# Graph attention with edges sorted on the chip: rows in a ring, earlier requests, scores by absolute values, sums per chunk and ScalarE weights in the last chunk

## Chip, core and metric

The kernel runs on one core of one Trainium2 chip. The metric is the device time of an execution in microseconds. Of the kernel before, three timed runs gave 5407.89, 5410.82 and 5411.46 us (median 5410.82). One more execution was profiled.

## What is computed

One graph-attention layer over 12,500 nodes of 128 features and 412,500 edges of 64 features. The core of the reference (biases, the layer norm ahead of it and the second norm behind it are left in one line each):

```
h0 = relu(layernorm(x))
h, q, k, v = h0 @ Wn, h0 @ Wq, h0 @ Wk, h0 @ Wv          # + biases
eh = edge_features @ We
hmid   = leaky_relu(concat([q[src], k[tgt], eh]) @ A1 + b1, 0.2)
scores = leaky_relu(hmid @ A2 + b2, 0.2)                   # 8 heads per edge
w   = softmax(scores.mean(-1), axis=0)                     # over ALL edges
out = segment_sum(w[:, None] * v[tgt], src)                # by source node
y = h + out
result = x + gamma * layernorm_core(y) + beta
```

The target nodes of the edges come sorted, the source nodes don't. The softmax runs over all edges at once, and the sum goes by source node.

## The kernel before

**Tiling.** Nodes lie in 98 blocks of 128. Edges lie in 403 groups of 8 tiles of 128, cut into four chunks of 121, 109, 98 and 75 groups (CHUNKS, line 62). For each chunk there is a table in HBM (`tabs`) in which every node block has 11, 10, 9 or 7 tiles of 128 edge rows; a row holds the place of its source node within the block, 128 hidden values and 128 values of v (ROW = 257 float32).

**First stage** (`first_stage`, line 757): for every group, matmuls make the rows of its edges (lines 809 and 812), ScalarE takes them out of PSUM into a ring of 16 rows (lines 792 and 795), and POOL stores them with indirect DMAs into the table at slots counted beforehand (line 747). Counting and placing (`count`, `plan`, `place_slots`) run beside the chunk before.

**Second stage** (`second_stage`, line 824): for every node block of a chunk,
- `load` (831): SP asks for the block's rows (`rows_of`, at most 11 tiles, a pool of BUFS = 6 buffers) and for `qw`, the block's query rows.
- `places` (839): PE transposes the places into `t_bank`; `put_places` (843): ScalarE makes them bytes (`plT`) and stores them to HBM; `spread_places` (850): SP loads them back broadcast to all partitions (`pls`); `select` (857): VectorE makes the one-hot matrix `sel_q`.
- per quad of 4 tiles, `turn` (864): PE transposes the hidden rows and adds the query part; `steep` (876): leaky ReLU, as ScalarE's `low` = 0.2 h (881) and VectorE's maximum (882), which writes back into `rows_of`.
- `heads_of` (885): PE multiplies by A2 into `s_ps`; `add_bias` (893): ScalarE, `z`; `by_slot` (898): VectorE's leaky ReLU of z (902) and its transpose (904); `scores` (906): `none` (910, marks empty slots), the sum over heads (912), score and its maximum (916).
- `spread_top` (919), `greatest` (928): the largest score so far, over all partitions; `exponentials` (933); `add_weights` (945): this block's sum, faded by the change of the maximum (948).
- `weights` (951): VectorE makes, for each tile, the matrix `w` with the edge's weight at its source's place (955); `products` (959): PE multiplies it with the v part (964); `add_sums` (967) adds the result into `acc` (971, 973).

**The order of the work.** PE, VectorE, ScalarE and SP each run in the order in which the instructions are written (a manual schedule), and `plan_of` (line 976 on) sets that order. A block of nq quads begins at step t = 2 i0, i0 being the number of quads before it: a block of 9 to 11 tiles has three quads and so six steps, a block of 7 tiles has two quads and four steps. Each job has a step relative to t and, within a step, a turn value. The products of a block run LAG = 11 steps behind its turns. Steps of the second stage are interleaved with those of the first stage of the next chunk (`interleave`, `some_steps`); the stage of chunk c's stores runs beside the second stage of chunk c - 1, and the second stage of the last chunk runs alone. SP's loads stand in the same order: a load whose wait isn't met stops all that are behind it.

**Setup.** Line 227 on: A2 and b2 are loaded and divided by 8; `b2_col` holds the bias at partitions 32 g to 32 g + 7. Line 246 on: src and dst are loaded (`raw_src`, `raw_dst`), and all slots come from them.

**End.** `all_sums` (1020) turns the per-block sums into one; the last lines normalize and store. `other_edges` (1035) treats edges that found no slot; there its loop runs zero times.

Of the kernel before, what the change touches and what calls it, by code (L numbers as in the profile page):

```python
# [10 lines left out]
FP = mybir.dt.float32  # L11
# [3 lines left out]
U8 = mybir.dt.uint8  # L15
AF = mybir.ActivationFunctionType
ALU = mybir.AluOpType
AX = mybir.AxisListType
# [4 lines left out]
P = 128  # L23
D = 128
DE = 64
H = 8
EPS = 1e-5
SLOPE = 0.2
# [5 lines left out]
QUAD = 4  # L34
LAG = 11

BUFS = 6

RROWS = 16

SPARE = 2

# [8 lines left out]
ROW = 2 * D + 1  # L51
# [60 lines left out]
def kernel(ctx: ExitStack, tc: tile.TileContext, n_edges, x, src, dst, ea, w_nv, w_qt, w_kt,  # L112
# [12 lines left out]
    nc = tc.nc  # L125
    NP = x.shape[0]
    NTN = NP // P
# [8 lines left out]
    for i, share in enumerate(CHUNKS):  # L136
        n = NG - g0 if i == len(CHUNKS) - 1 else max(1, round(NG * share))
# [4 lines left out]
    NC = len(chunks)  # L142
    most_tiles = max(ct for _, _, ct, _ in chunks)

    blocks = []
# [24 lines left out]
    late = ctx.enter_context(tc.tile_pool(name="late", bufs=1))  # L170
# [60 lines left out]
    nc.vector.memset(b2_col, 0.0)  # L231
    for g in range(4):
        nc.scalar.dma_start(out=b2_col[32 * g:32 * g + H, :], in_=b2.rearrange("a h -> h a"))
    nc.vector.tensor_scalar(a2_sb, a2_sb, 1.0 / H, None, op0=ALU.mult)
    nc.vector.tensor_scalar(b2_col, b2_col, 1.0 / H, None, op0=ALU.mult)


    w_ea = const.tile([P, 2, D], FP, name="w_ea")
    cp = ctx.enter_context(tc.tile_pool(name="count", bufs=2))
# [410 lines left out]
    sums_of = late.tile([P, NTN], FP, name="sums_of")  # L650
    nc.vector.memset(sums_of, 0.0)

    def newest(top_of, old, new, pool):

# [169 lines left out]
    def second_stage():  # L824


        rows_of, qws, plss, state = {}, {}, {}, {}
        state["s_ps"] = ps_s.tile([P, 512], FP, name="s_ps")
        nc.vector.memset(state["s_ps"], 0.0)

        def load(i):
            c, b, ct, _, _ = blocks[i]
            rows_of[i] = pb.tile([P, most_tiles, ROW], FP, name="rows_of")
            nc.sync.dma_start(out=rows_of[i][:, 0:ct, :],
                              in_=tabs[c % 2][b * ct * P:(b + 1) * ct * P, :].rearrange("(p j) r -> p j r", p=P))
            qws[i] = ps.tile([P, 3 * D], BF, name="qw")
            nc.sync.dma_start(out=qws[i], in_=q_tab.rearrange("(p t) d -> t p d", p=P)[b])
# [4 lines left out]

        def put_places(i):
            ct = blocks[i][2]
            plT = p3.tile([most_tiles, P], U8, name="plT")
            nc.scalar.activation(plT[:ct, :], t_bank[:ct, 0:P], AF.Copy)
            at = i % 4 * most_tiles
            nc.scalar.dma_start(out=pl_d[at:at + ct, :], in_=plT[:ct, :])
# [49 lines left out]
        def by_slot(i):  # L898

            n = 32 * blocks[i][2]  # L900
            z = state["z"][:, 0:n]
            nc.vector.scalar_tensor_tensor(z, z, SLOPE, z, op0=ALU.mult, op1=ALU.max)
            state["zt"] = p3.tile([P, most_tiles * 32], FP, name="zt")
            nc.vector.transpose(state["zt"][:, 0:n], z)
# [28 lines left out]
        def exponentials(i):  # L933
            c, b, ct, _, _ = blocks[i]
            score = state["score", i][:, 0:ct]
            less = less_of[c % 2][:, b:b + 1]
            if c == 0:
                nc.scalar.activation(score, score, AF.Exp, bias=less, accum_out=sums_of[:, b:b + 1])  # L938
            else:
                state["part", i] = ps.tile([P, 1], FP, name="part_of")  # L940
                nc.scalar.activation(score, score, AF.Exp, bias=less, accum_out=state["part", i])
# [3 lines left out]
        def add_weights(i):  # L945
            c, b, _, _, _ = blocks[i]
            if c > 0:
                nc.vector.scalar_tensor_tensor(sums_of[:, b:b + 1], sums_of[:, b:b + 1], state["fade", i],
                                               state.pop(("part", i)), op0=ALU.mult, op1=ALU.add)

        def weights(i, q):
            state["w", i, q] = ws = []
            for t in range(q * QUAD, min((q + 1) * QUAD, blocks[i][2])):
                w = pw.tile([P, P], FP, name="w")
                nc.vector.tensor_scalar(w, iota_f, rows_of[i][:, t, 0:1], state["score", i][:, t:t + 1],  # L955
                                        op0=ALU.is_equal, op1=ALU.mult)
                ws.append(w)

        def products(i, q):
            ct = blocks[i][2]  # L960
# [17 lines left out]
        def at(when, turn_, job, *args):  # L978
            plan_of.setdefault(when, []).append((turn_, len(plan_of[when]) if when in plan_of else 0, job, args))

        for i, (c, b, ct, nq, i0) in enumerate(blocks):
            t = 2 * i0
            at(load_at(i), 2, load, i)
            first = t - 9 if nq > 2 else t - 8
            at(first, 3, places, i)
            at(first + 1, 0, put_places, i)
            at(first + 3, 0, spread_places, i)
            at(t - 1, 3, select, i)
            for q in range(nq):
# [12 lines left out]
            for q in range(nq):  # L1002
                at(t + 2 * q - 1, 0, weights, i, q)
                at(t + 2 * q, 1, products, i, q)
            at(t + 2 * nq - 1, 0, add_sums, i)
        for when in range(min(plan_of), max(plan_of) + 1):
            for _, _, job, args in sorted(plan_of.get(when, []), key=lambda j: j[:2]):
                job(*args)
            yield

    def load_at(i):

        _, _, _, nq, i0 = blocks[i]
        t = 2 * i0 - (17 if nq > 2 else 11)
        if i >= BUFS:
            _, _, _, nq, i0 = blocks[i - BUFS]
            t = max(t, 2 * (i0 + nq - 1) + LAG)
        return t

    def all_sums():  # L1020

        less = less_of[(NC - 1) % 2]
        most_of = late.tile([P, NTN], FP, name="most_of")
        nc.vector.tensor_scalar(most, less[:, NTN - 1:NTN], -1.0, None, op0=ALU.mult)
        nc.scalar.activation(most_of, less, AF.Exp, bias=less[:, NTN - 1:NTN], scale=-1.0)
        nc.vector.tensor_mul(sums_of, sums_of, most_of)
        nc.vector.tensor_reduce(sums, sums_of, AX.X, ALU.add)
        return most_of

    def count_left():  # L1030
# [4 lines left out]
    def other_edges(most_of):  # L1035

        with tc.tile_pool(name="others", bufs=1) as op, tc.tile_pool(name="others_ps", bufs=1, space=PSUM) as ops_:
            turns = nc.values_load(trips[0:1, NC:NC + 1], min_val=0, max_val=NG, skip_runtime_bounds_check_because=BECAUSE)
            with tc.For_i(0, turns, 1) as g:  # L1039
                b2_bc = op.tile([P, H], FP, name="b2_bc")  # L1040
                nc.sync.dma_start(out=b2_bc, in_=b2.to_broadcast([P, H]))
                nc.vector.tensor_scalar(b2_bc, b2_bc, 1.0 / H, None, op0=ALU.mult)
# [53 lines left out]
                nc.vector.scalar_tensor_tensor(z, z, SLOPE, z, op0=ALU.mult, op1=ALU.max)  # L1096
                sc = op.tile([P, SUPER], FP, name="sc")
                nc.vector.tensor_reduce(sc, z, AX.X, ALU.add)
                none = op.tile([P, SUPER], FP, name="none_n")
                nc.vector.tensor_scalar(none, flag, 1e30, -1e30, op0=ALU.mult, op1=ALU.add)  # L1100
                nc.vector.tensor_add(sc, sc, none)
# [23 lines left out]
    for c in range(NC + 1):  # L1125
# [16 lines left out]
        if c == 0:  # L1142
# [3 lines left out]
                    pass  # L1146
            clear_rest(1)
            setup.close()
            pb = main.enter_context(tc.tile_pool(name="pb", bufs=BUFS))
# [97 lines left out]
```

## Time and profile before

| what | value |
|---|---|
| median of three timed runs | 5410.82 us |
| the profiled execution | 5393.0 us |
| its span, first to last instruction | 5391.3 us |
| busy share of the span: PE, DVE, ACT, POOL | 78%, 78%, 40%, 63% |
| mean granted TensorE clock | 0.921 |
| L747 indirect stores on POOL | 3223, 3343.9 us, mean 1038 ns |
| L955 weights on VectorE | 3626, 1037.2 us, mean 356 ns |
| L902 leaky ReLU of z on VectorE | 392, 180.5 us, mean 461 ns |
| L948 faded sums on VectorE | 294, 64.8 us, mean 220 ns |
| L881 `low` on ScalarE | 1078, 569.0 us, mean 528 ns |
| moved by DMA | 1309.97 MB, mean 243 GB/s |

How to read it: an engine's busy time is the union of its instructions, so durations of instructions that overlap add up to more. A group's idle time is what its engine waited ahead of it, with the releaser behind the arrow. "issue" is idle time in which nothing that the profile shows was waited for. In the timeline the columns are start, duration, engine, line and operation; "x3" merges three neighbours. Shares over the whole span hide the stages, which have different limits, so tables by window are read first. Waits of SP (SPq) are those of the queue that issues the loads.

### The profile page before, as it was taken

What the parts mean: (1) busy time and instruction counts of PE and PEld (TensorE: products, weight loads), DVE (VectorE), ACT (ScalarE), POOL (GpSimd) and SP (SyncE); (2) the same over time, 40 slices, a digit from 0 to 9 for tenths busy, and PEclk for the clock granted to TensorE, in tenths of its full rate; (3) what the DMA queues carried; (4) which work ended last, traced back from release to release, by engine and by line L of the source; (5) the groups of instructions that cost most, each with busy time, mean ns of one, the idle gap of its engine ahead of it and who ended that gap; (6) DMA issues with size and microseconds to landing.
All of it is one profiled execution on the core that took longest, in us unless ns stands there. A gap on an engine that the chain in (4) does not pass through costs nothing. (4 is left out here: it accounts for less than half of the span.)

```text
span 5391.3 us, 90152 instructions
## 1 busy us (share of the span) xinstructions
PE 4218.1 (78%) x26817; PEld 2951.6 (55%) x27160; DVE 4204.3 (78%) x13299; ACT 2160.8 (40%) x6046; POOL 3379.1 (63%) x3261
## 2 busy tenths in 40 slices
PE   4777766565588888998788888987888888878782
PEld 2344433333266666666566666665666666655551
DVE  7777754544378888888788988887877788799889
ACT  1344422222244444444344444443444444434333
POOL 0477777777677777777667777777666666500002
PEclk8788887777789999999999999999999999999996
DMA  8677765555489999888789999988899998755554
GB/s 244 201 234 228 230 196 162 169 164 167 162 262 290 280 280 282 279 281 281 251 257 284 289 284 282 282 286 260 263 284 280 276 287 284 242 194 193 190 194 164
DMA packets 609678, 1309.97 MB, mean 243 GB/s; under 512 B 117392, under 2 KB 371524, under 8 KB 571168
## 3 DMA queue, kind: packets, MB, share of 16 engines
q1 hardware_dynamic: 404312, 841.81, 53.1%
q0 software_dynamic: 154704, 424.26, 21.8%
q10 hardware_dynamic: 50168, 38.07, 2.2%
q8 instruction: 218, 3.57, 0.3%
q14 instruction: 276, 2.26, 0.1%
HBM read 782.14 MB, written 521.60 MB: 242 GB/s over the span
## 5 line engine op out<-in xcount | busy, mean ns | idle before, releaser
L747 POOL DMA_INDIRECT tab<-row,slots x3223 | 3343.9, 1038 | 1339.5 <-issue 702.8
L809 PE MATMUL row_ps<-w_ea,ea_t 128*128 128x256 f32 x3224 | 1105.0, 427 | 379.2 <-ACT row L795 311.5
L964 PE MATMUL o_ps<-rows_of,w 128*128 128x128 f32 x7252 | 1073.6, 287 | 127.9 <-DVE w L955 125.7
L964 PEld LDWEIGHTS o_ps<-rows_of,w 128*128 128x128 f32 x7252 | 954.8, 193 | 254.7 <-DVE w L955 199.7
L795 ACT ACTIVATE row<-row_ps 128x512 f32<-128x512 f32 x1612 | 939.6, 590 | 279.7 <-PE row_ps L812 215.7
L955 DVE TENSOR_SCALAR w<-iota_f,rows_of,score 128x128 f32<-128x128 f32 x3626 | 1037.2, 356 | 0.8 <-ACT score L938 0.8
L809 PEld LDWEIGHTS row_ps<-w_ea,ea_t 128*128 128x128 f32 x3224 | 577.9, 208 | 680.9 <-ACT row L795 397.7
L881 ACT ACTIVATE low<-h_ps 128x512 f32<-128x512 f32 (+3 forms) x1078 | 569.0, 528 | 848.7 <-PE h_ps L873 690.8
L873 PE MATMUL h_ps<-sel_q,qw 128*128 128x512 bf16 (+3 forms) x2891 | 753.7, 344 | 60.1 <-DVE sel_q L861 40.2
L882 DVE TENSOR_TENSOR rows_of<-h_ps,low 128x512 f32<-128x512 f32 (+3 forms) x1078 | 648.2, 601 | 134.7 <-ACT low L881 121.3
L812 PE MATMUL row_ps<-kv,sel 126*128 126x256 bf16 x3224 | 666.3, 290 | 1.5 <-DVE sel L785 1.5
L792 ACT ACTIVATE row<-place 128x4 f32<-128x4 bf16 x806 | 166.9, 207 | 1219.5 <-DMA tab<-row,slots 1195.7
L870 PE MATMUL h_ps<-ident,rows_of 128*128 128x128 f32 x3626 | 592.9, 279 | 0.0
L450 DVE TENSOR_TENSOR one<-bins_b,block 128x500 f16<-128x500 bf16 x646 | 301.5, 467 | 326.8 <-PE run L457 322.8
L812 PEld LDWEIGHTS <-sel 126*128 126x128 bf16 x3224 | 337.6, 105 | 279.3 <-issue 55.0
L870 PEld LDWEIGHTS h_ps<-ident,rows_of 128*128 128x128 f32 x3626 | 433.1, 143 | 102.2 <-issue 39.5
L503 DVE TENSOR_REDUCE num<-run 128x5 f32<-128x500 f32 x646 | 433.4, 671 | 11.8 <-PE run L457 11.8
L861 DVE TENSOR_SCALAR sel_q<-pls,part 128x1408 bf16<-128x1408 uint8 (+3 forms) x392 | 330.6, 843 | 108.5 <-DMA pls<-pl_d 108.0
L1174 POOL TENSOR_TENSOR xt<-xt,affine 128x640 f32<-128x640 f32 (+1 forms) x20 | 32.7, 1649 | 608.2 <-DMA xt<-in_x 595.4
L873 PEld LDWEIGHTS <-qw 128*128 128x128 bf16 x3234 | 314.9, 99 | 160.7 <-issue 54.6
L889 PE MATMUL s_ps<-rows_of,a_sb 128*32 128x352 f32 (+3 forms) x3136 | 292.2, 444 | 117.2 <-DVE rows_of L882 116.1
L457 PE MATMUL run<-one,rest_b 128*128 128x500 f16 x642 | 268.9, 419 | 145.1 <-DVE num L503 143.9
(195 smaller groups left out, 4161.9 us busy)
## 6 DMA issues: line engine op xcount, KB each, us to landing
rows_of<-tab SPq DMA_DIRECT2D x98, 1413.5 KB
rows_of<-tab SPq DMA_DIRECT2D x98, 1285.0 KB
rows_of<-tab SPq DMA_DIRECT2D x98, 1156.5 KB
ea_t<-in_ea SPq DMA_DIRECT2D x403, 256.0 KB
rows_of<-tab SPq DMA_DIRECT2D x98, 899.5 KB
tab<-row,slots POOLq DMA_INDIRECT x3223
offs<-off_d SPq DMA_DIRECT2D x403, 126.0 KB
tab<-blank SPq DMA_DIRECT2D x196, 257.0 KB
```

The lines of the kernel that those rows point to most:

```text
L503: nc.vector.tensor_reduce(num, strips[:, :, :m].rearrange("p b m -> p m b"), AX.X, ALU.max)
L747: i = nc.gpsimd.indirect_dma_start(out=tabs[c % 2][:, :], out_offset=bass.IndirectOffsetOnAxis(ap=slots[c][t // (8 * STR)][:m, t % (8 * ST ...
L795: nc.scalar.activation(row[:, :, 1:ROW], bank, AF.Copy)
L809: nc.tensor.matmul(bank[:, :, 0:D], lhsT=ea_g[:, ts(k, P)], rhs=w_ea, start=True, stop=False, skip_group_check=True)
L812: nc.tensor.matmul(bank[:, b, :], lhsT=sel[:, ts(b * halves + k, P)], rhs=kv, start=False, stop=True, skip_group_check=True)
L861: nc.vector.tensor_scalar(sel[:, 0:n], plss[i][:, 0:n], part1, None, op0=ALU.is_equal)
L870: nc.tensor.matmul(h_ps[:, ts(j, P)], lhsT=rows_of[i][:, q * QUAD + j, 1:D + 1], rhs=ident, is_transpose=True, start=j == 0, stop=False, s ...
L873: nc.tensor.matmul(h_ps[:, 0:m * P], lhsT=qws[i][:, ts(k, D)], rhs=plss[i][:, q * QUAD * P:(q * QUAD + m) * P], start=False, stop=k == 2, ...
L881: nc.scalar.activation(low, h_ps, AF.Copy, scale=SLOPE)
L882: nc.vector.tensor_max(rows_of[i][:, q * QUAD:q * QUAD + m, 1:D + 1], h_ps.rearrange("p (j e) -> p j e", j=m), low.rearrange("p (j e) -> p ...
L955: nc.vector.tensor_scalar(w, iota_f, rows_of[i][:, t, 0:1], state["score", i][:, t:t + 1], op0=ALU.is_equal, op1=ALU.mult)
L964: nc.tensor.matmul(state["o_ps"][:, 0:D], lhsT=w, rhs=rows_of[i][:, t, D + 1:ROW], start=t == 0, stop=t == ct - 1)
```

## The change

1. Rows of the second stage lie in one tile of 66 tile places, `held`, used as a ring, instead of six buffers of 11 tiles: 66 places hold 6 blocks of 11 or 10 tiles, 7 of 9, 9 of 7. `load_at` asks for them at step -19 (three quads) or -17 (two quads), not before the places are free, instead of -17 or -11.
2. `places` goes to step -11 and `put_places` to -10 for all blocks (from -9 and -8, or -8 and -7); `spread_places` goes to -6 (three quads, as before) or -7 (two quads, from -5). `plT` gets two buffers.
3. The leaky ReLU of the scores is replaced: with slope s, the sum over heads of leaky(z) equals (1-s)/2 times [sum of |z| + (1+s)/(1-s) times sum of z]. A2 and b2 are scaled by (1-s)/2 and get a ninth column H with the second sum, so VectorE's L902 goes, the sum over heads takes absolute values, and one addition of column H to `none` comes in. The bias column is now made from a row by a matmul into `t_bank`.
4. Softmax sums: each block's sum is kept, and they are joined once per chunk (`sum_chunk`) instead of once per block (L948).
5. In the last chunk the weights of tiles 1, 3 and 5 of a block's 7 are made by ScalarE in two activations, |iota - place| and then relu(score - 4 |iota - place|).
6. For blocks of two quads `heads_of` moves from step t-1 (turn value 3) to step t (turn value 2, behind the next block's first turn), and all jobs from `add_bias` to `exponentials` come one step later; t is the step behind the last turn.

The diff, cut to its core:

```diff
-BUFS = 6
+RING = 66
+PEAKS = (1, 3, 5)
...
+    bend, line = (1.0 - SLOPE) / 2.0, (1.0 + SLOPE) / (1.0 - SLOPE)
+    nc.vector.tensor_scalar(a2_sb, a2_sb, bend / H, None, op0=ALU.mult)
+    nc.vector.tensor_reduce(a2_sb[:, H:H + 1], a2_sb[:, 0:H], AX.X, ALU.add)
+    nc.vector.tensor_scalar(a2_sb[:, H:H + 1], a2_sb[:, H:H + 1], line, None, op0=ALU.mult)
...
+    with tc.tile_pool(name="bias_row", bufs=1) as bp:
+        b2_row = bp.tile([1, 4, 32], FP, name="b2_row")
+        nc.vector.memset(b2_row, 0.0)
+        for g in range(4):
+            nc.scalar.dma_start(out=b2_row[:, g, 0:H], in_=b2)
+        nc.vector.tensor_scalar(b2_row, b2_row, bend / H, None, op0=ALU.mult)
+        nc.vector.tensor_reduce(b2_row[:, :, H], b2_row[:, :, 0:H], AX.X, ALU.add)
+        nc.vector.tensor_scalar(b2_row[:, :, H], b2_row[:, :, H], line, None, op0=ALU.mult)
+        nc.tensor.matmul(t_bank[:, 0:1], lhsT=b2_row.rearrange("p g h -> p (g h)"), rhs=ones[0:1, 0:1], start=True, stop=True)
+        nc.vector.tensor_copy(b2_col, t_bank[:, 0:1])
...
+    def sum_chunk(c, most_in):
+        less = less_of[c % 2]
+        nc.scalar.activation(most_in, less, AF.Exp, bias=less[:, NTN - 1:NTN], scale=-1.0)
+        if c > 0:
+            fade = late.tile([P, 1], FP, name="fade_sums")
+            nc.scalar.activation(fade, less_of[1 - c % 2][:, NTN - 1:NTN], AF.Exp, bias=less[:, NTN - 1:NTN], scale=-1.0)
+        nc.vector.tensor_mul(sums_of[c % 2], sums_of[c % 2], most_in)
+        part = late.tile([P, 1], FP, name="part_sums")
+        nc.vector.tensor_reduce(part if c > 0 else sums, sums_of[c % 2], AX.X, ALU.add)
+        if c > 0:
+            nc.vector.scalar_tensor_tensor(sums, sums, fade, part, op0=ALU.mult, op1=ALU.add)
...
+        held = pb.tile([P, RING, ROW], FP, name="rows_of")
...
-            rows_of[i] = pb.tile([P, most_tiles, ROW], FP, name="rows_of")
+            rows_of[i] = held[:, place_of[i]:place_of[i] + ct, :]
...
-            plT = p3.tile([most_tiles, P], U8, name="plT")
+            plT = p3.tile([most_tiles, P], U8, name=f"plT{i % 2}")
...
-            nc.vector.scalar_tensor_tensor(z, z, SLOPE, z, op0=ALU.mult, op1=ALU.max)
...
-            nc.vector.tensor_reduce(summed, state["zt"][:, 0:32 * ct].rearrange("p (t h) -> p t h", h=32)[:, :, 0:H],
-                                    AX.X, ALU.add)
+            zt = state["zt"][:, 0:32 * ct].rearrange("p (t h) -> p t h", h=32)
+            nc.vector.tensor_reduce(summed, zt[:, :, 0:H], AX.X, ALU.add, apply_absolute_value=True)
+            nc.vector.tensor_add(none, none, zt[:, :, H])
...
+                if blocks[i][0] == NC - 1 and t in PEAKS:
+                    nc.scalar.activation(w, iota_f, AF.Abs, bias=rows_of[i][:, t, 0:1], scale=-1.0)
+                    nc.scalar.activation(w, w, AF.Relu, bias=state["score", i][:, t:t + 1], scale=-4.0)
+                    continue
...
-            first = t - 9 if nq > 2 else t - 8
+            first = t - 11
...
-            at(first + 3, 0, spread_places, i)
+            at(first + (5 if nq > 2 else 4), 0, spread_places, i)
...
-            at(t - 1, 3, heads_of, i)
+            if nq > 2:
+                at(t - 1, 3, heads_of, i)
+            else:
+                at(t, 2, heads_of, i)
+                t += 1
...
-            at(t + 4, 3, add_weights, i)
+            if b == NTN - 1 and c < NC - 1:
+                at(t + 4, 4, add_weights, c)
...
-        t = 2 * i0 - (17 if nq > 2 else 11)
-        if i >= BUFS:
-            _, _, _, nq, i0 = blocks[i - BUFS]
-            t = max(t, 2 * (i0 + nq - 1) + LAG)
-        return t
+        t = 2 * blocks[i][4] - (19 if blocks[i][3] > 2 else 17)
+        return t if free_at[i] is None else max(t, free_at[i])
```

`place_of` and `free_at` are worked out ahead of the run: blocks follow one another in the ring, a block that doesn't fit at its end starts at place 0, and `free_at` is the step of the last products of the blocks that it covers.

More of the change, by code (lines that the diff above doesn't have):

```diff
@@ L649 @@
     nc.vector.memset(nothing, 1e30)
-    sums_of = late.tile([P, NTN], FP, name="sums_of")
-    nc.vector.memset(sums_of, 0.0)
+    sums_of = [late.tile([P, NTN], FP, name=f"sums_of{c}") for c in range(2)]
+    def sum_chunk(c, most_in):
[9 more added lines that the diff above has]
+            nc.vector.scalar_tensor_tensor(sums, sums, fade, part, op0=ALU.mult, op1=ALU.add)
     def newest(top_of, old, new, pool):
@@ L832, in load @@
             c, b, ct, _, _ = blocks[i]
-            rows_of[i] = pb.tile([P, most_tiles, ROW], FP, name="rows_of")
-            nc.sync.dma_start(out=rows_of[i][:, 0:ct, :],
+            rows_of[i] = held[:, place_of[i]:place_of[i] + ct, :]
+            nc.sync.dma_start(out=rows_of[i],
                               in_=tabs[c % 2][b * ct * P:(b + 1) * ct * P, :].rearrange("(p j) r -> p j r", p=P))
@@ L900, in by_slot @@
             n = 32 * blocks[i][2]
-            z = state["z"][:, 0:n]
-            nc.vector.scalar_tensor_tensor(z, z, SLOPE, z, op0=ALU.mult, op1=ALU.max)
             state["zt"] = p3.tile([P, most_tiles * 32], FP, name="zt")
-            nc.vector.transpose(state["zt"][:, 0:n], z)
+            nc.vector.transpose(state["zt"][:, 0:n], state["z"][:, 0:n])
         def scores(i):
@@ L936, in exponentials, with add_weights @@
             less = less_of[c % 2][:, b:b + 1]
[L937 to L941, printed above, removed]
+            nc.scalar.activation(score, score, AF.Exp, bias=less, accum_out=sums_of[c % 2][:, b:b + 1])
+            if c > 0:
                 state["fade", i] = ps.tile([P, 1], FP, name="fade_of")
                 nc.scalar.activation(state["fade", i], less_of[1 - c % 2][:, b:b + 1], AF.Exp, bias=less, scale=-1.0)
[L945 to L949, printed above, removed]
+        def add_weights(c):
+            sum_chunk(c, p3.tile([P, NTN], FP, name="most_in"))
         def weights(i, q):
@@ L1009, in second_stage @@
             yield
-    def load_at(i):
-        _, _, _, nq, i0 = blocks[i]
-        t = 2 * i0 - (17 if nq > 2 else 11)
-        if i >= BUFS:
-            _, _, _, nq, i0 = blocks[i - BUFS]
-            t = max(t, 2 * (i0 + nq - 1) + LAG)
-        return t
+    place_of, owner_of, free_at = [], [None] * RING, []
+    for i, (_, _, ct, _, _) in enumerate(blocks):
+        at = place_of[-1] + blocks[i - 1][2] if i else 0
+        if at + ct > RING:
+            at = 0
+        place_of.append(at)
+        free_at.append(max((2 * (blocks[j][4] + blocks[j][3] - 1) + LAG for j in owner_of[at:at + ct] if j is not None),
+                           default=None))
+        owner_of[at:at + ct] = [i] * ct
+    def load_at(i):
+        t = 2 * blocks[i][4] - (19 if blocks[i][3] > 2 else 17)
+        return t if free_at[i] is None else max(t, free_at[i])
     def all_sums():
@@ L1024, in all_sums @@
         nc.vector.tensor_scalar(most, less[:, NTN - 1:NTN], -1.0, None, op0=ALU.mult)
-        nc.scalar.activation(most_of, less, AF.Exp, bias=less[:, NTN - 1:NTN], scale=-1.0)
-        nc.vector.tensor_mul(sums_of, sums_of, most_of)
-        nc.vector.tensor_reduce(sums, sums_of, AX.X, ALU.add)
+        sum_chunk(NC - 1, most_of)
         return most_of
@@ L1098, in other_edges @@
                 nc.vector.tensor_reduce(sc, z, AX.X, ALU.add)
+                nc.vector.tensor_scalar(sc, sc, 1.0 / bend, None, op0=ALU.mult)
                 none = op.tile([P, SUPER], FP, name="none_n")
```

11 lines of the change are left out of this document (3 added, 8 removed).

## Prediction

> **What bounds the kernel now.** I read the table by stage first. Indirect stores L747 start for chunks 0 to 3 at 175.7, 1466, 2676 and 3781 us and end at 4686; from then on only the second stage of chunk 3 runs, to 5300. Rows: window, us, then PE, PEld, DVE, ACT, POOL busy, granted clock, DMA share, GB/s.
>
> ```profile
> 1466.00:2662.00 1196.00, 1053.26 (x7037) 764.25 (x7130) 1014.63 (x3115) 515.96 (x1320) 919.47 (x870) 0.97 0.89 278
> 2676.00:3765.00 1089.00, 962.60 (x6642) 710.00 (x6737) 941.22 (x3016) 503.01 (x1367) 827.83 (x783) 0.98 0.89 277
> 3781.00:4686.00 905.00, 796.54 (x5657) 592.05 (x5757) 723.45 (x2353) 432.08 (x1236) 622.32 (x599) 0.99 0.90 278
> 4720.00:5280.00 560.00, 448.43 (x3448) 321.58 (x3493) 504.53 (x1885) 223.96 (x659) 1.31 (x1) 0.99 0.58 193
> ```
>
> The first two stages belong to POOL: besides its busy time it sits about 0.30 us in "issue" ahead of most stores, so 919 + 870 x 0.30 = 1180 of 1196 us are gone, and 828 + 783 x 0.30 = 1063 of 1089. The third is not full on POOL (622 + 180 = 802 of 905) nor on PE (797). The waits of SP's queue and of VectorE, and one block in the timeline, show its limit:
>
> ```profile
> SPq L854 <- DMA pl_d<-plT: 539.0, 98, 8.6
> ...
> DVE sel_q L861 <- DMA pls<-pl_d: 100.4, 79, 2.8
> ```
>
> ```profile
> 4403.22 0.27 PE L841 MATMUL t_bank<-ident,rows_of 128*9 128x128 f32 x1
> ...
> 4405.75 0.27 ACTq L848 DMA_DIRECT2D pl_d<-plT  x1
> ...
> 4410.94 0.35 SPq L854 DMA_DIRECT2D pls<-pl_d  x1
> ...
> 4416.53 0.85 DVE L861 TENSOR_SCALAR sel_q<-pls,part 128x1152 bf16<-128x1152 uint8 x1 [1.52 <-DMA pls<-pl_d]
> ```
>
> From a block's places (L841) to its selection (L861) takes 13.3 us: 5.2 for the small store to land, 5.6 for the broadcast load. The plan puts 8 steps between them, a block has 6, so a block can't take less than 13.3 x 6/8 = 10.0 us when it goes like this one, about 9.2 on the mean (905/98). This latency is the third stage's limit.
>
> In the last stage a block takes 560/94 = 5.96 us (94 of L941 in that window). Its limit is a loop as well:
>
> ```profile
> 5002.71 0.33 SPq L834 DMA_DIRECT2D rows_of<-tab  x1
> ...
> 5007.30 0.27 PE L841 MATMUL t_bank<-ident,rows_of 128*7 128x128 f32 x1 [0.58 <-DMA rows_of<-tab]
> ...
> 5008.27 0.33 SPq L834 DMA_DIRECT2D rows_of<-tab  x1
> ```
>
> ```profile
> SPq L834 <- PE o_ps L964: 387.8, 92, 6.6
> ```
>
> A load is issued when the products of the block six before free its buffer; 4.6 us later L841 has it, then come those products (0.83 us) and the next load: 5.56 us. VectorE is close behind, 504.53/94 = 5.37 us a block; PE needs 4.77, ScalarE 2.38.
>
> **Last stage, what is taken away.** With 66 places in the ring a 7-tile block may be asked for at step -17 instead of -11, six steps ahead of its transposes instead of three: the rows loop goes. VectorE loses L902 (0.42 from start to start), L948 (0.13) and three of seven L955 (0.257 each, 0.77); the added sum of `none` and column H is not in the trace: nearest is L912's step of 0.24 ahead of a dependent; I take 0.22, ends 0.11 and 0.42 (L902). VectorE needs 5.37 - 1.32 + 0.22 = 4.27 us a block. ScalarE gains six activations of 128x128; the nearest row, L1196, has 299 ns: 2.38 + 1.8 = 4.2 us. By busy time PE would be next at 4.77.
>
> **Last stage, what the new order costs.** For blocks of two quads `heads_of` moves behind the next block's first turn, and bias, scores, top and exponentials one step later. By the plan's steps each engine then has, per block: PE products q0 (4), spread_top, turn q0, heads_of, products q1, places, turn q1; VectorE greatest, sel_q, w w, max q0, transpose, none, summed, sum, score, acc, w w, max q1; ScalarE places, low q1, two activations, exp, fade, z, low q0, four activations. That closes a loop through three engines, once per block. From the start of sel_q (starts to next starts, in this trace):
>
> ```profile
> 5004.74 0.68 DVE L861 TENSOR_SCALAR sel_q<-pls,part 128x896 bf16<-128x896 uint8 x1
> ...
> 5004.88 0.60 PE L889 MATMUL s_ps<-rows_of,a_sb 128*32 128x224 f32 x8 [0.25 <-DVE rows_of L882]
> ...
> 5005.55 0.45 ACT L896 ACTIVATE z<-s_ps,b_col 128x224 f32<-128x224 f32 x1 [0.52 <-PE s_ps L889]
> ...
> 5006.76 0.60 ACT L881 ACTIVATE low<-h_ps 128x512 f32<-128x512 f32 x1 [0.76 <-PE h_ps L873]
> ```
>
> sel_q 0.68 and a hand-over 0.05 (0.73); three L873 to the next matmul 0.65 (1.38); L889 to z 0.67 (2.05); z less its overlap 0.36 (2.41); low 0.60 and 0.05 (3.06); L882 0.60 (3.66); L904 0.34, L910 0.11, L912 0.13, the new sum 0.22, L916 0.09 (4.55); acc 0.26 (4.81); the first w 0.34 and 0.05 (5.20); four products, 0.22 each (6.08); L921 0.27 and 0.05 (6.40); greatest to the next sel_q 0.27: **6.67 us**. Today the same path is broken twice: heads stand ahead of the turn, so z is ready while VectorE still makes w, and spread_top stands ahead of the products. In the new order VectorE idles some 2 us per block behind sel_q, since only two w's are left to cover PE's 0.65 + 0.67 and ScalarE's 0.36 + 0.60. So 6.67 - 5.96 = +0.71, times 98: **+70 us**. By the ends of the new sum (0.11 to 0.42) the loop is 6.56 to 6.87: +59 to +89.
>
> **Third stage.** Places go to step -11, the store to -10, the broadcast stays at -6: ten steps instead of eight, and plT has two buffers. The loop becomes 13.3 x 6/10 = 8.0 us in the block shown. Next are POOL (802/98 = 8.2) and PE (8.1); VectorE also loses L902 and L948 for the sum, about 0.35 a block. Two floors lie together there, and the landings may get slower when transfers come sooner; between 8.2 and 9.23 I take the middle, 8.7: **-52 us** (ends 0 and -100).
>
> A rule of the Trainium skill can be held against this: in "DMA: Bandwidth & Descriptors", Anatomy of one DMA, a transfer has about 2.0 us fixed besides its bytes. By it the small store would land 3.2 us sooner, the chain would be 10.1 us, 7.6 a block, and would bind nothing: the stage would save 0 and the sum would be 52 us higher. The trace has 5.2 us for that landing; it decides.
>
> **First two stages.** VectorE's 0.35 a block is cover, since POOL is full. What POOL idles beyond "issue" is some 90 + 107 us of the two; I take **-8**, ends -40 and +10. The turn from one chunk to the next costs more: asked for at -19, the new chunk's first rows stop SP until the stores land (SP stood from 2652.3 to 2666.5 before), and now the broadcast of the block two before (step -18) is behind it, as are three groups' loads. I put 4 us on each of two changes: **+8** (0 to 16).
>
> **Start and end.** The row for the bias lies where raw_src comes to lie, so the load at 0.81 us must wait for the small loads, three VectorE operations and a matmul. The last of the small loads was issued at 3.49; with landing and these, 6 to 8 us. About 2 us of small casts that stood between the long ones come ahead: **+4** (0 to 8). Setup of a2, sums per chunk and the end: nothing; three chunk sums of five small operations are about 1 us each, beside POOL.
>
> **Sum**: +4 - 8 + 8 - 52 + 70 = +22 us. The profiled execution took 5393.0 us (span 5391.3), so 5415; the median of the runs is 5410.82, 17.8 above it, so 5433. A measurement here can tell about 0.2%, 11 us, from no change.
>
> **Rivals.**
> - A (forecast), 5433, own range 5391 to 5476. Chance 0.50.
> - B: the third stage is held by the transfers themselves and saves nothing: 5411 + 4 + 8 + 70 = 5493. For it: DMA share 0.89 to 0.90 and 277 to 278 GB/s in all three stages, whatever bounds them. Against it: SP stood 539 of 905 us waiting for a store of 1.1 KB, with nothing to issue. 0.18.
> - C: the loop isn't as long as summed and the last stage stays near 5.96 us, while the third gains: 5411 + 4 - 8 + 8 - 52 = 5363. It would need 0.7 us of the chain to overlap, for instance z ahead of the turn's matmuls. 0.18.
> - D, the other side: faster. The last stage falls to PE's 4.77 us: 98 x 1.19 = -117, so 5246. It decides if VectorE finds other work behind sel_q than I see. For it: VectorE is the fullest engine there (504.53 of 560), and it is relieved by 1.1 us. Against it: the loop of 6.67, in which that relief is what uncovers the wait. 0.14. The Trainium skill ("Perfetto Trace Analysis", Identifying the Most-Contended Engine) speaks for it: the engine with the highest occupancy is to be optimized first. No run here shows yet whether that holds when the order changes with it.
>
> The range 5350 to 5500 takes in A, B and C and leaves D out. Faster by over 0.2%: D, most of C, a little of A, 0.33; within 0.2%: 0.11; slower: 0.56.
>
> **What would show it.** In the last stage of the changed kernel: a block of about 6.7 us; VectorE busy near 4.3 of it, idle ahead of max (L882's successor) on ScalarE's low, ScalarE idle ahead of z on PE; no wait of L841 for rows and no wait of SP for products. If VectorE's share there stays near 90%, the loop is wrong. In the third stage: the wait of sel_q for pls nearly gone, SP's wait for pl_d cut by half, 8.7 us a block; at 9.2 B holds. raw_src issued at 6 to 8 us. POOL's durations in the first two stages unchanged at 1.057 us.

## The result, and the profile after

The changed kernel takes 5442.32 us (median of 4 runs, 5432.2 to 5445.48) where the kernel before takes 5409.35 us beside it (4 runs): ratio 1.006, 95% interval 1.0043 to 1.0078. It is slower, by 33 us. The profiled execution took 5432.2 us, span 5430.4. First the table by stage of the changed kernel; windows go from the first to the last indirect store of a chunk, the fourth lies in the last stage. Here, as in the expectations below, "second stage" is the stretch of chunk 1's stores (first row) and "third stage" that of chunk 3's (third row). Columns: window, us, then PE, PEld, DVE, ACT, POOL busy, granted clock, DMA share, GB/s.

```profile
1467.00:2651.00 1184.00, 1052.52 (x7118) 760.44 (x7116) 976.41 (x3104) 521.56 (x1319) 912.94 (x872) 0.96 0.88 281
2664.00:3755.00 1091.00, 967.61 (x6738) 708.71 (x6736) 896.06 (x2921) 501.84 (x1367) 836.51 (x784) 0.98 0.87 276
3770.00:4640.00 870.00, 788.40 (x5729) 591.06 (x5728) 659.87 (x2241) 417.92 (x1236) 616.86 (x599) 0.99 0.90 289
4720.00:5280.00 560.00, 397.44 (x3047) 268.36 (x3046) 354.96 (x1321) 349.71 (x1073) 0.00 (x0) 1.00 0.59 168
```

The second stage is shorter (1197.6 us before, 1183.5 now, from its first store to its last), the third too (904.6 to 869.4), and what follows the last store is longer: 705.7 to 790.6. In the last row VectorE has fallen from 504.53 to 354.96 us of 560 and PE from 448.43 to 397.44: every engine but ScalarE does less in the same time. One block of that stage in the timeline (start, duration, engine, line; in brackets the idle time ahead and what ended it):

```profile
5003.28 0.68 DVE L886 TENSOR_SCALAR sel_q<-pls,part 128x896 bf16<-128x896 uint8 x1
...
5004.01 0.81 PE L898 MATMUL h_ps<-sel_q,qw 128*128 128x512 bf16 x3 [0.61 <-DVE sel_q L886]
...
5004.75 0.59 PE L914 MATMUL s_ps<-rows_of,a_sb 128*32 128x224 f32 x8
...
5005.41 0.45 ACT L921 ACTIVATE z<-s_ps,b_col 128x224 f32<-128x224 f32 x1 [1.38 <-PE s_ps L914]
5005.76 0.59 ACT L906 ACTIVATE low<-h_ps 128x512 f32<-128x512 f32 x1
...
5006.38 0.69 DVE L907 TENSOR_TENSOR rows_of<-h_ps,low 128x512 f32<-128x512 f32 x1 [1.91 <-ACT low L906]
...
5008.49 1.16 PE L986 MATMUL o_ps<-rows_of,w 128*128 128x128 f32 x8 [1.36 <-DVE w L978]
...
5009.48 0.27 PE L945 MATMUL s_ps<-ident,top_of 128*128 128x128 f32 x1
...
5009.79 0.36 DVE L954 TENSOR_SCALAR_CACHE_REDUCE s_ps<-s_ps,less_of 128x128 f32<-128x128 f32 x1 [0.37 <-PE s_ps L945]
...
5010.07 0.68 DVE L886 TENSOR_SCALAR sel_q<-pls,part 128x896 bf16<-128x896 uint8 x1
```

The reader can go around it: sel_q, PE's matmuls with it, heads, z, low, max, then transpose, scores, acc and w (not shown), products, the top's transpose, greatest, and the next sel_q, 6.79 us later. The long waits follow one another along this way, 0.61, 1.38, 1.91 and 1.36 us, each for the step just ahead of it; what else the waiting engine has to do stands behind the wait in its order. The waits of the whole window say the same (waited for: us in all, times, longest):

```profile
DVE rows_of L907 <- ACT low L906: 173.7, 165, 1.9
PEld o_ps L986 <- DVE w L978: 143.1, 82, 1.8
ACT z L921 <- PE s_ps L914: 114.7, 83, 1.4
```

The third stage, waits of SP's queue and of VectorE:

```profile
SPq L879 <- DMA pl_d<-plT: 363.5, 80, 8.1
...
DVE s_ps L954 <- PE s_ps L945: 110.7, 98, 2.7
DVE sel_q L886 <- DMA pls<-pl_d: 50.4, 26, 5.2
```

SP's wait for the small store fell from 539.0 to 363.5 us, sel_q's for the broadcast from 100.4 to 50.4. PE is now busy 788 of 870 us there (797 of 905 before), and most of the 82 it lacks are waits for w (44.4) and sel_q (30.2). PE is the fullest engine; that it alone is the limit isn't shown, since sel_q still waits for the broadcast.

### The profile page after: what moved, and what is told of

The parts are those of the page before. It is cut to its first block, busy times and chain, and to the rows that moved or that the text cites. A ratio compares the mean times of both kernels' runs of the same rounds, so it can differ in the third digit from the quotient of the medians.

```text
span 5430.4 us, 90109 instructions
## 1 busy us (share of the span) xinstructions
PE 4219.5 (78%) x27162; PEld 2932.1 (54%) x27162; DVE 3960.3 (73%) x12724; ACT 2336.2 (43%) x6640; POOL 3374.2 (62%) x3261
## 5 line engine op out<-in xcount | busy, mean ns | idle before, releaser
L986 PEld LDWEIGHTS o_ps<-rows_of,w 128*128 128x128 f32 x7252 | 933.3, 192 | 457.0 <-DVE w L978 385.5
L978 DVE TENSOR_SCALAR w<-iota_f,rows_of,score 128x128 f32<-128x128 f32 x3332 | 954.8, 352 | 0.0
L898 PE MATMUL h_ps<-sel_q,qw 128*128 128x512 bf16 (+3 forms) x3234 | 772.7, 348 | 94.9 <-DVE sel_q L886 74.1
L921 ACT ACTIVATE z<-s_ps,b_col 128x352 f32<-128x352 f32 (+3 forms) x392 | 199.0, 508 | 642.2 <-PE s_ps L914 640.6
```

The costliest lines, as they stand in the source:

```text
L898: nc.tensor.matmul(h_ps[:, 0:m * P], lhsT=qws[i][:, ts(k, D)], rhs=plss[i][:, q * QUAD * P:(q * QUAD + m) * P], start=False, stop=k == 2, ...
L986: nc.tensor.matmul(state["o_ps"][:, 0:D], lhsT=w, rhs=rows_of[i][:, t, D + 1:ROW], start=t == 0, stop=t == ct - 1)
```

## The experiments

Kernels of one group ran on one chip, beside the kernel before. Its own median was 5409, 5356, 5347 and 5361 us in the four groups, so kernels are compared by ratio, and by stages of their profiles. "Us a block" is the mean distance of sel_q's starts in the last stage without the first and last five; the second and third stage go from the first store of chunk 1 or 3 to its last. Each stage length is from one profile, and kernels that are alike in a stage differ there: the third stage takes 853.8 to 870.8 us in the seven profiles that have both the ring and the earlier places, and 883.5 to 904.6 in the seven others.

| kernel | median us | ratio to before, 95% | second stage | third stage | us a block, last stage |
|---|---|---|---|---|---|
| before | 5409.35 | 1 | 1197.6 | 904.6 | 5.95 |
| changed | 5442.32 | 1.0060 (1.0043 to 1.0078) | 1183.5 | 869.4 | 6.80 |
| e1_heads_back | 5303.50 | 0.9905 (0.9882 to 0.9928) | 1180.8 | 860.7 | 5.61 |
| e2_no_act_weights | 5437.78 | 1.0151 (1.0129 to 1.0173) | 1182.5 | 870.8 | 6.90 |
| e3_heads_alone | 5534.95 | 1.0335 (1.0313 to 1.0356) | 1196.8 | 890.5 | 7.61 |
| e4_low_first | 5334.31 | 0.9961 (0.9947 to 0.9974) | 1180.1 | 854.4 | 5.91 |
| c_before | 5352.73 | 1.0010 (1.0000 to 1.0020) | 1193.1 | 890.2 | 5.91 |
| c_after | 5421.43 | 1.0144 (1.0127 to 1.0161) | 1184.6 | 853.8 | 6.80 |
| e5_put_later | 5250.86 | 0.9815 (0.9798 to 0.9831) | 1182.7 | 866.2 | 5.03 |
| e6_six_blocks | 5859.97 | 1.0953 (1.0934 to 1.0971) | 1184.3 | 889.0 | 11.18 |
| e7_ring_alone | 5365.88 | 1.0011 (1.0000 to 1.0021) | 1191.5 | 886.5 | 5.83 |
| e8_places_late | 5446.33 | 1.0168 (1.0151 to 1.0185) | 1182.3 | 883.5 | 6.80 |
| e9_no_act_weights | 5281.77 | 0.9860 (0.9843 to 0.9876) | 1181.9 | 865.4 | 5.27 |
| e10_scores_alone | 5350.74 | 0.9981 (0.9968 to 0.9993) | 1188.1 | 889.5 | 5.92 |

**e1_heads_back.** **The changed kernel with the heads back ahead of the next turn.**

```diff
-            if nq > 2:
-                at(t - 1, 3, heads_of, i)
-            else:
-                at(t, 2, heads_of, i)
-                t += 1
+            at(t - 1, 3, heads_of, i)
```

> The changed kernel with one part undone: for blocks of two quads heads_of goes back ahead of the next block's first turn, and bias, scores, top and exponentials go back one step; ring, earlier requests, absolute values and ScalarE's six activations stay. Theory (the moved heads close the loop): the 6.79 us a block of the last stage falls to between 5.3 and 5.6, the sum of its durations on the fullest chain left (ScalarE's low, its weight activations, the second low, VectorE's max, heads, the next turn); 98 blocks by 1.2 to 1.5 us are 118 to 147, so 5442 falls to 5295 to 5325. Rival 1 (ScalarE's 128x128 activations, at 0.39 to 0.40 us each, are what made the stage longer): no gain, 5430 to 5450. Rival 2 (the ring and the earlier requests disturb the transfers of the last stage): no gain either, 5430 to 5450.

Measured: 5.61 us a block, 0.9905 of before. All other parts of the change are in it, ScalarE's activations too, and the last stage is 1.18 us a block quicker than the changed kernel's: rivals 1 and 2 fall. What holds the 5.61 is read in its timeline:

```profile
5003.35 0.49 ACT L906 ACTIVATE low<-h_ps 128x384 f32<-128x384 f32 x1 [0.40 <-DVE s_ps L954]
...
5003.88 0.56 DVE L907 TENSOR_TENSOR rows_of<-h_ps,low 128x384 f32<-128x384 f32 x1 [0.70 <-ACT low L906]
...
5004.49 0.59 PE L914 MATMUL s_ps<-rows_of,a_sb 128*32 128x224 f32 x8 [0.69 <-DVE rows_of L907]
...
5006.36 0.60 ACT L906 ACTIVATE low<-h_ps 128x512 f32<-128x512 f32 x1 [0.76 <-DVE none L937]
...
5008.31 0.25 ACT L871 ACTIVATE plT<-t_bank 7x128 uint8<-7x128 f32 x1
...
5008.59 0.27 ACTq L873 DMA_DIRECT2D pl_d<-plT  x1
...
5008.96 0.49 ACT L906 ACTIVATE low<-h_ps 128x384 f32<-128x384 f32 x1 [0.40 <-DVE s_ps L954]
```

The way is low, max, heads, the turn's matmuls, the next low, four weight activations (5006.85 to 5008.31), plT and the issue of its store, and low again: 5.61 us. The profile puts the last wait down to DVE L954, but PE's matmuls for this low had ended about 5007.9 and L954's work isn't read by it; what stood ahead of low on ScalarE was the issue of the store.

**e2_no_act_weights.** **All weights on VectorE, the new order kept.**

```diff
-PEAKS = (1, 3, 5)
+PEAKS = ()
```

> The changed kernel with all of the last chunk's weights on VectorE again (PEAKS empty), the new order of the heads kept. Theory of the loop: ScalarE's activations lie beside it, and the two more weights on VectorE stand in it between two waits, so the stage stays at 6.8 to 6.9 us a block: 5440 to 5455. Rival (ScalarE's activations are the cost): the stage falls back to the 5.96 us of before, 98 by 0.83 = 81 us less, 5360.

Measured: 6.90 us a block. Without a single weight on ScalarE the stage stays as long (6.80 with them), so those activations aren't its cost.

**e3_heads_alone.** **The kernel before with the heads moved alone** (the first diff, the other way round).

> The kernel before with one part of the change alone: heads_of behind the next block's first turn for blocks of two quads, and what follows it one step later. Theory of the loop: with all weights on VectorE and the two operations that the change removes still in the chain the loop is 6.9 to 7.3 us a block against 5.96, so 92 to 131 us over before: 5500 to 5540. Rival 1 (the loop appears only with ScalarE's weights, since only two weights are then left on VectorE to cover the matmuls): 5.96 stays, 5410. Rival 2 (the new order is what gains something and another part is the cost): below 5400.

Measured: 7.61 us a block and 1.0335. The mean block is 0.3 us above the loop expected, and the kernel takes 179 us more than before beside it (5356.31) instead of 92 to 131. A usual block in its timeline takes 7.38 us (sel_q at 5001.50 and 5008.88); others are slower, and the mean granted clock of the window is 0.95 (more on that at the end). The move alone costs 3%; both rivals fall. VectorE's wait is the same one:

```profile
DVE rows_of L882 <- ACT low L881: 114.3, 61, 2.7
```

**e4_low_first.** **One link of the loop cut: low ahead of z on ScalarE.**

```diff
-            at(t, 0, add_bias, i)
+            at(t, 0 if nq > 2 else 1, add_bias, i)
```

> The changed kernel with two ScalarE operations exchanged in the last chunk: low of the next block's first quad ahead of the bias activation z, nothing else. Theory of the loop: z (0.36 us, and its wait of 1.4 us for the heads) leaves the chain from sel_q to max; by the durations in its trace the loop falls from 6.79 to about 6.0 us a block, 98 by 0.8 = 78 less: 5345 to 5380. Rival (busy time or transfers set the stage, not this order): 5430 to 5450.

Measured: 5.91 us a block, near the 6.0 expected. The time, 5334.31 us, lies 11 us below the expected range; its third stage is 15 us shorter than the changed kernel's first profile (854.4 against 869.4), but e2 on the same chip has 870.8, so this is spread and not the chip. Two operations exchanged on one engine, with no work added or removed, take 0.89 us a block away: z stood in the loop ahead of low. The rival falls.

**c_before, c_after.** **Both kernels again, on one chip.**

> The kernel before, unchanged, profiled beside the next three, because its times differ from one call to the next by more than a per cent (5409 in one, 5356 in another). Theory: its last stage is bound by the loop through a load of rows (issue, landing, transposes, products, next load), so only that stage may differ where transfers land sooner or later: 5.4 to 6.0 us a block, the stages ahead of it alike. Rival: all stages are shorter or longer alike.

> The changed kernel, unchanged, profiled beside the others. Theory: its last stage is bound by the loop of three engines, which holds no transfer, so it has 6.79 us a block again, wherever it runs: 5430 to 5445, and the ratio to before is larger where the kernel before is quicker. Rival (a transfer is in its loop too): its last stage shortens together with that of before.

Of the changed kernel the theory held for the last stage: 6.80 us a block again. Its time, 5421.43 us, lies below the 5430 expected. The third stage is 36.4 us shorter than c_before's. Of the kernel before both the theory and the rival fell: its last stage is the same on both chips (5.95 and 5.91), and it is the chunk stages that differ, the third by 14 us. By stages, first to last, the two profiles of this pair differ by +39.7 us and those of the first pair by +39.1; the medians differ by 74 and 33 us. The last stage gives +85 us in both pairs, so the medians would leave -11 and -52 us for what stands ahead of it. In this pair the profiled run of c_before is the slowest of its ten and that of c_after the fastest of its four, so its profiles show more gain there than its medians do. Why the chunk stages vary so is open.

**e5_put_later.** **Heads back, and the places put later.**

```diff
-            at(first + 1, 0, put_places, i)
+            at(first + (1 if nq > 2 else 2), 0 if nq > 2 else 3, put_places, i)
```

> The first experiment (heads back ahead of the turn) with one thing more: for blocks of two quads the places are put (plT and its store) one step later, behind the second low, the exponential and the fade instead of ahead of the second low. Theory: with the heads back, the loop of 5.61 us runs through ScalarE: low, two weights in four activations, plT, the issue of its store (0.33 with its hand-over), the second low, then VectorE's max, heads, the next turn. Without plT and the issue it is 5.61 less 0.60, 5.0 us a block, PE's busy 4.7 being next: 98 by 0.6 = 58 us below the first experiment, 5240 to 5255. Rival (PE or a transfer holds the 5.61): no gain, 5295 to 5310.

Measured: 5.03 us a block, 5250.86 us, 0.9815: it beats both kernels. The reading of the loop in e1 holds, the rival falls. In its last stage PE is the fullest engine now, 389.54 of 420 us:

```profile
4720.00:5140.00 420.00, 389.54 (x3081) 283.31 (x3078) 356.07 (x1333) 352.86 (x1083) 2.44 (x2) 1.00 0.72 226
```

**e6_six_blocks.** **The same with six blocks again.**

```diff
-        at = place_of[-1] + blocks[i - 1][2] if i else 0
-        if at + ct > RING:
+        at = place_of[-1] + most_tiles if i else 0
+        if at + most_tiles > RING:
...
-        t = 2 * blocks[i][4] - (19 if blocks[i][3] > 2 else 17)
+        t = 2 * blocks[i][4] - (19 if blocks[i][3] > 2 else 11)
```

> The one before (e5_put_later) with the ring undone: places in steps of 11 tiles, so six blocks again, and the rows of a block of two quads asked for at step -11. Theory: the loop through the load comes back, because a load then has to wait for the products of the block six before: 5.4 to 6.0 us a block as in the kernel before, 98 by 0.4 to 1.0 = 40 to 98 us above e5_put_later, 5285 to 5345, and the chunk stages hardly differ. Rival (rows were never the limit, the order of VectorE's work was): as e5_put_later, 5240 to 5255.

Measured: 11.18 us a block, far outside both. The edit put the request for rows into the step in which the changed kernel transposes their places (-11), where the kernel before has three steps between. PE then stands at the head of its queue until the rows land, and all of the block's work behind it:

```profile
5008.89 0.83 PE L986 MATMUL o_ps<-rows_of,w 128*128 128x128 f32 x6
5014.36 0.38 PE L866 MATMUL t_bank<-ident,rows_of 128*7 128x128 f32 x1 [4.64 <-DMA rows_of<-tab]
```

So it doesn't test the loop through the load as meant. It does show that places at step -11 can't be had without rows asked for earlier, and that in the third stage the earlier places give nothing without the seventh block of the ring: 889.0 us, where e5 with the ring has 866.2 and c_before 890.2 on the same chip.

**e7_ring_alone.** **The kernel before with the ring alone** (`held`, `place_of` and `load_at` as in the change, with -17 for both kinds of block).

> The kernel before with the ring alone: 66 places, and the rows of a block of two quads asked for at step -17; order, places, scores and weights as before. Theory: in the last stage the loop through the load of rows goes, and VectorE's busy time of 5.37 us a block is next: 5.4 to 5.6 instead of 5.9, 98 by 0.3 to 0.5 = 30 to 50 us below before; the other stages stay. Rival (the wait for the load only looked like the limit, an order like that of the heads holds 5.9): as before.

Measured: 5.83 us a block, 1.0011: the 30 to 50 us expected didn't come, as the rival had it. Waits of SP in the last stage, the kernel before of the second pair and this one:

```profile
SPq L834 <- PE o_ps L964: 364.2, 87, 6.6
SPq L854 <- DMA pl_d<-plT: 11.8, 17, 1.1
```

```profile
SPq L855 <- DMA pl_d<-plT: 377.9, 85, 7.8
```

The wait for products is gone and the same 370 us are a wait for the small store. A block's way from its places to its selection in this kernel:

```profile
5005.53 0.27 PE L842 MATMUL t_bank<-ident,rows_of 128*7 128x128 f32 x1
...
5006.51 0.27 ACTq L849 DMA_DIRECT2D pl_d<-plT  x1
...
5011.20 0.32 SPq L855 DMA_DIRECT2D pls<-pl_d  x1
...
5015.69 0.68 DVE L862 TENSOR_SCALAR sel_q<-pls,part 128x896 bf16<-128x896 uint8 x1
```

It takes 10.2 us for seven steps (-8 to -1), and a block has four: 10.2 x 4/7 = 5.8 us. It is the reading of the third stage, made for the last: a second loop lay right behind the first. That this one holds the 5.83 is read from the waits; it wasn't isolated.

**e8_places_late.** **The changed kernel with the places late for blocks of three quads.**

```diff
-            first = t - 11
+            first = t - 9 if nq > 2 else t - 11
...
-            at(first + (5 if nq > 2 else 4), 0, spread_places, i)
+            at(first + (3 if nq > 2 else 4), 0, spread_places, i)
```

> The changed kernel with the earlier places undone for blocks of three quads: transposes at step -9, store at -8, broadcast at -6 as before; the rest stays. Theory: the third stage goes back to its 880 to 893 us from the 843 to 858 of the changed kernel, 35 us, so 5455 to 5475; the second stage stays where the changed kernel has it, since POOL bounds it. Rival 1 (VectorE's relief is what shortened the third stage): 5420 to 5440, as the changed kernel. Rival 2 (the earlier places also gave the 9 to 14 us of the second stage): another 9 to 14 us more, with the second stage back at 1193 to 1198.

Measured: third stage 883.5 us, where e9 of the same group, alike in that stage but for the places, has 865.4, and e7 and e10 of that group, whose places are late too, have 886.5 and 889.5. So the earlier places give 18 us there, and 13 to 30 by the spread of the seven profiles that have them and the ring; 35 were expected. The 843 to 858 us that the expectation gives the changed kernel aren't what its two profiles show, 869.4 and 853.8, and the time, 5446.33 us, lies below the expected 5455. The second stage stays at 1182.3: rival 2 falls. Rival 1 falls too, since VectorE is relieved here (and in e10) and the stage stays long. Chunk 2's stage is a little longer with the earlier places: 1089.5 to 1095.7 us in the eight profiles that have them, 1082.0 to 1088.9 in the six that don't.

**e9_no_act_weights.** **e5_put_later with all weights on VectorE** (PEAKS empty).

> The fifth experiment (e5_put_later) with all weights on VectorE again. Theory: VectorE then needs 4.3 + 0.77 = 5.1 us a block and, with its waits, 5.2 to 5.35 instead of 5.03; 98 by 0.2 to 0.3 = 20 to 30 us above e5_put_later, 5270 to 5285. Rival (ScalarE's weights give nothing even with the heads back): as e5_put_later, 5245 to 5255.

Measured: 5.27 us a block, 0.24 more than e5, 0.9860 against 0.9815. As expected, with the loops gone ScalarE's weights are worth some 24 us; in the changed kernel (e2) only 0.1 us a block came of them.

**e10_scores_alone.** **The kernel before with joined scores and sums per chunk alone** (the changed kernel with parts 1, 2, 5 and 6 undone).

> The kernel before with the joined scores and the sums per chunk alone (six buffers' worth of places, rows, places, heads and weights as before). They take 0.42 + 0.13 us off VectorE and add 0.20 in each block. Theory: in the last stage VectorE isn't the limit of the kernel before, the load of rows is, so 5.9 us a block stays and VectorE's busy share falls; the second stage, where POOL is full, changes by less than 10 us: 5335 to 5360 in all, next to before. Rival (VectorE, busy 90% of the last stage, is its limit): 98 by 0.35 = 34 us less there, and as much again in the third stage.

Measured: 5.92 us a block, 0.9981. VectorE fell from 413.97 to 385.62 of 460 us in the last stage (c_before and this kernel) and the stage stayed: the rival falls. It followed the rule that rival D leaned on: the Trainium skill ("Perfetto Trace Analysis", Identifying the Most-Contended Engine) has the engine with the highest occupancy optimized first. Here that engine was relieved and the last stage gained nothing (5.91 and 5.92 us a block), because it wasn't the limit.

## Why the prediction was right

5433 was forecast, 5442 came, and the mechanism is the one of case A. That the number came so near is in part luck: the two large terms were 15 and 17 us too low, and the small ones together 15 too high. By the profiles the change costs 39 us instead of 22; the medians come nearer because the profiled run of the kernel before lies 17.8 us below its median and that of the changed kernel 10.1.

- **Last stage**, +70 forecast, +84.9 measured. The loop is 6.79 us instead of 6.67. Two terms were small: from PE's three matmuls to the next 0.74 instead of 0.65, four products 0.99 instead of 0.88; the others were together 0.08 less. VectorE 354.96/82.5 = 4.30 us a block (4.27 forecast). That the moved heads are the cost is shown from both sides: taken out (e1, 1.18 us a block less), added alone (e3, 1.7 more), and cut at one link (e4, 0.89 less). The other parts give back 0.34 us a block (5.95 in the kernel before, 5.61 in e1). Rivals C and D fail on the 6.79 us; D's reason, relief of the fullest engine, fails on e10 too.
- **The step that failed** in this part: that today's limit is the loop through the rows, and that it goes with the ring. It goes, but next to nothing is gained by it alone (e7, 5.91 to 5.83). The view that shows the small store in the third stage wasn't read for the last one. It did no harm to the sum, since the earlier places came with the ring, and with both the stage gets down to 5.03 (e5).
- **Third stage**, -52 forecast, -35.2 and -36.4 measured, 8.87 us a block. Three signs came short: SP's wait was cut by a third, not by half, sel_q's for the broadcast by half and not nearly to nothing, and the middle between 8.2 and 9.23 was too hopeful. The two readings behind that middle are weak. Over the whole stage the way from L841 to L861 takes 13.1 us on the mean; times 6/8 that is 9.8, but a block took 9.2, so "can't take less" is too strong. And POOL's 8.2 counts 0.30 us of issue ahead of every store, where the trace has 120.5 us for all 599, which makes 743 of 905 us or 7.6 a block. What holds the stage at 8.87 now isn't shown; PE is the fullest engine there. Ring and earlier places belong together here as well: each without the other leaves 883.5 to 889.0 us, as c_before with neither (890.2), and both give 853.8 to 870.8. Rival B fails: the stage gained, and it moved 289 GB/s, above the 278 of before. The Trainium skill's 2.0 us that the prediction held against this stage stand in that section ("DMA: Bandwidth & Descriptors", Anatomy of one DMA) for transfers that GpSimd issues; this store is issued by ScalarE, and the 5.2 us of the trace were rightly preferred.
- **First two stages** (stores of chunks 1 and 2), -8 forecast: -12.1 in the first pair of profiles, +0.5 in the second. Chunk 1's became shorter (14.2 and 8.5 us), chunk 2's longer (2.0 and 9.0). The prediction's 1180 of 1196 us for POOL counts issue ahead of all 870 stores; the trace has 199.3 us in 650, so about 1119, and the idle time of some 90 us that it names further down fits that. Stores keep their length (912.94/872 = 1.047 and 836.51/784 = 1.067 us).
- **Turns between chunks**, +8 forecast: from a chunk's last store to the next one's first 13.3, 12.6 and 15.8 us before and 13.2, 13.1 and 15.8 after. No cost.
- **Start**, +4 forecast: raw_src is issued at 5.89 us instead of 0.81, and the first store comes 1.3 us later in the first pair, 3.6 us sooner in the second. No cost that can be told.

## What to carry to other kernels

When a step is moved in a hand-written order, go around the loop that it may close, engine by engine, from start to start, and compare that with the longest busy time; removing work from the fullest engine also removes the cover of its waits. A limit read from a wait has to be looked for in every stage, and the next one behind it too: in the third stage a longer ring and earlier places were each worth next to nothing alone, and both together some 23 us (863 against 886 on the mean). A small reorder (heads back, the store's issue behind the second low) turned a change that cost 0.6 to 1.4% into one that gains 1.9%.

## What the hardware showed

- In e6, PE stood 4.8 us for rows in every block (198.3 us in 41 waits of the last window below), and its matmuls afterwards were slow. Its windows: one wait, the 2.6 us behind the wait of the block before, and the stage (columns as in the first table):

```profile
5009.80:5014.30 4.50, 0.00 (x0) 0.00 (x0) 1.38 (x4) 1.27 (x4) 0.00 (x0) 0.72 0.65 227
5002.40:5005.00 2.60, 2.53 (x11) 2.02 (x12) 0.29 (x2) 0.49 (x1) 0.00 (x0) 0.50 0.00 0
...
4720.00:5180.00 460.00, 262.26 (x1517) 194.13 (x1517) 177.61 (x656) 180.66 (x533) 0.00 (x0) 0.79 0.32 101
```

  The granted clock is 0.50 right behind the wait, and the eight matmuls of four products take 1.91 us where the changed kernel's take 1.16. The Trainium skill ("TensorE: Matmul & The Clock Gate", Part 1: The HAM clock gate) says that PE falls to half its clock after an idle window of about 3.4 us; the trace of e6 agrees. Waits of 1.4 us, as in the changed kernel, leave the clock at 1.00. But in e3 PE never idles longer than 1.9 us in the last stage, and still its clock falls to 0.50 for 3.4 us at a time (once 6.8), 17 times between 4720 and 5280 us; there the measurement decides. One of these stretches, in the trace of e3:

```profile
4992.70:4996.10 3.40, 2.98 (x15) 1.13 (x14) 1.73 (x6) 0.58 (x3) 0.00 (x0) 0.50 0.19 52
```

  Which idle time is enough isn't shown by these runs.
- ScalarE's two activations of 128x128 take 393 and 402 ns in the changed kernel, where 299 had been taken from L1196. The Trainium skill ("ScalarE: Activation LUTs", What ACT_TABLE_LOAD costs) gives 280 ns and 0.833 ns an element for a bias that is a column. The estimate from these figures of the Trainium skill for 128 elements is 387 ns, with which the trace agrees to within 4%.
